# Key-tile order for the transposed image: packed reads for k and v, raster order restored in q's copy

## The chip, the cores and the metric

The kernel runs on one core of one Trainium2 chip. The metric is the device time of one execution in microseconds. A core has a matrix engine (TensorE, PE in the profile, with its weight loads listed as PEld), a vector engine (VectorE, DVE), an activation engine (ScalarE, ACT), a general engine (GpSimd, POOL) and SyncE (SP), which issues DMAs. Each engine works through its own queue in order; semaphores join them. A matmul takes a stationary operand, loaded into the array by its own instruction (LDWEIGHTS), and a moving operand that streams through; the result goes to PSUM[...].

## The reference

Eight images of 32 x 32 tokens with 384 channels go through two layers. Only the first layer is touched by the change; cut to what matters:

```python
# layer 0: group norm, then attention with 6 heads of 64 channels over all 1024 tokens of an image
qkv = gn(x).reshape(b, 1024, 384) @ qkv_w + qkv_b            # q, k, v per head
attn = (q * 64 ** -0.5) @ k.T                                # 1024 x 1024 per head
attn[h, w, h2, w2] += (q[h, w] . Rh[h, h2]) + (q[h, w] . Rw[w, w2])   # relative positions
x = x + (softmax(attn) @ v) @ proj_w + proj_b
# layer 1: x = x + causal attention(layer_norm(x)), then x = x + ffn(layer_norm(x))
```

The FFN quantises in groups along the batch, and only images 0 to 4 are in a group: images 5, 6 and 7 take no FFN. In softmax attention the order of the keys does not matter, as long as k, v and the position terms use the same one. The order of the queries shows in the output, and the position terms of layer 0 are made from q in raster order.

## The kernel before

**Stages.** Images are worked one after the other in `ORDER` = 5, 0, 1, 2, 3, 4, 6, 7. For each: group norm of the transposed image `gnT` (channels on partitions, 1024 tokens along the free side; `load_T`, `group_norm_T`), `layer0` (q, k, v, position tables), `attend0_fast` (scores, exponentials, values), the projection, then `attention1` and, for images 0 to 4, `ffn`. The time of a group norm of the next image, and of its first two thirds of q, falls into the layers of the current one: `ffn` calls `project_qk` for the image that follows, so that images 1, 2, 3, 4 and 6 find the results of q for the first two head pairs in PSUM. A tile framework puts buffers and semaphores in; the order on each engine is the order in the code, bent by `issue_after`, `behind_of` and `in_turn` (which chains matmuls).

**Keys in key tiles.** A tile of 128 keys is not 128 neighbours in raster order. Tokens are grouped in 256s, and tile (g, n) holds the tokens g * 256 + 2 * i + n, i from 0 to 127: the even or the odd columns of eight rows. This fits the position terms: `unit` and `r` (L913 to L916) add both terms of a tile with one matmul per head.

**q.** `queries_keys(m)` (L716 to L732), for m = 0 to 2, copies two halves of 512 tokens from PSUM to `q`, with scale and bias: half 0 on ACT (L732), half 1 on DVE (L730); in the first image both are on ACT. `tables` (L738) multiplies q with the relative positions (L746), in raster order. `spread` and `place` (L760, L786) bring the tables by DMA and by two DVE subtractions (L794) to the rows `r`; of the DMAs of L800 half are issued by SP, half by POOL.

**k and v.** They are made by 15 products each instead of 18 (`ProductSet`, L612): each product multiplies a sum of image parts with a sum of weight parts (`xf`, `wf`), 128 channels by 512 tokens, and adds into one of six PSUM banks A to F. Some of the partial states are copied by ACT to SBUF pages `u` (L643, L647), four are combined there (L663), and when a bank is full, `final` adds or subtracts the kept part and writes the result: `put_keys` (L822 to L825) for k, `put_values` (L827 to L829) for v, both on DVE. For k the weights are stationary and 512 tokens stream. For v the roles are turned, since v is wanted with keys on partitions: the image tile is stationary and the weights `wf` stream, four tiles of 128 keys per product (`tiles=by_keys`, L633 to L636). In the profile the matmuls of both carry L578 and the names f_pr_A to f_pr_F; those of v have `wf` first. Layer 1 makes its q and v by the same products (f_pr_1q, f_pr_1v), with tiles of 128 neighbouring tokens.

As the image lies in raster order, key tiles are gathered with a step of two tokens where v reads it:

```python
def by_keys(x):
    keys = x.rearrange("p (g i n) -> p g n i", g=2, n=2)
    return [keys[:, j // 2, j % 2] for j in range(4)]
```

and `put_keys` sorts k into key tiles when it writes, so that the scores (L909) read packed tiles of k. Its innermost step goes over n, 128 elements of 4 bytes apart.

**The first image.** POOL makes the sums of layer 1's weights (`layer1_forms`, L197 to L219) in two parts. The second is issued after the last DMA of `place` that POOL issues for head pair 0 (L991 to L993). After v's products a small activation (L865) reads one of the pages and opens the exponentials (L918 to L920); the scores take PSUM banks as `put_values` gives them free.

Of the kernel before, what the change touches and what calls it, by code (L numbers as in the profile page):

```python
# [19 lines left out]
P = 128  # L20
B, H, W, C = 8, 32, 32, 384
T = H * W
NJ = T // P
NC = C // P
# [67 lines left out]
def conv_attn_hybrid(  # L92
# [19 lines left out]
    nc = tc.nc  # L112
# [21 lines left out]
    wqkv_sb = wf.rearrange("p r s o -> p (r s o)")[:, : NC * 3 * C].rearrange("p (k o) -> p k o", k=NC)  # L134
# [286 lines left out]
    def stages(pools):  # L421
# [151 lines left out]
        def behind_of(ins):  # L573
            return contextlib.nullcontext() if ins is None else tc.issue_after(ins)
# [111 lines left out]
        def project_qk(b, xT, m, w):  # L686

            made = [pools.o_tile(f"qk_{b}_{m}_{half}") for half in range(2)]
            for half in range(2):
                for i in range(NC):  # L690
                    (in_turn if pools.fast else nc.tensor.matmul)(
                        made[half], w[:, i, ts(m, P)], xT[:, i, ts(half, 512)], start=(i == 0), stop=(i == NC - 1)
                    )
            return made

        def layer0(b, xT):


            q, k = (pools.image(f"{n}_{b}") for n in ("q", "k"))
# [16 lines left out]
            def queries_keys(m):  # L716
                p = m % NPAIR
                bias = bqk[:, m : m + 1]
                made = ahead.pop((b, m)) if (b, m) in ahead else project_qk(b, xT, m, plain[0])
                for half, ps in enumerate(made):  # L720
                    t = ts(half, 512)
                    if m < NPAIR:
                        dst = q[:, p, t]
                    else:
                        dst = k[:, p, t].rearrange("d (g n i) -> d g i n", n=2, i=P)
                        ps = ps.rearrange("d (g i n) -> d g i n", n=2, i=P)
                    scale = qscale if m < NPAIR else 1.0
                    if half and not (pools.fast and b == ORDER[0]):
                        with behind_of(last_ended[0] if pools.fast else None):
                            last_ended[0] = nc.vector.tensor_scalar(dst, ps, scale, bias, ALU.mult, ALU.add).ins  # L730
                    else:
                        nc.scalar.activation(dst, ps, AF.Identity, bias=bias, scale=scale)  # L732
# [76 lines left out]

            v = pools.flat(f"v0_{b}")[:, : NJ * C].rearrange("p (j c) -> p j c", j=NJ)  # L810

            keys = xT.rearrange("p k (g i n) -> p k g n i", n=2, i=P)

            def values(j):
                ps = pools.o_tile(f"v0_{b}_{j}")[:, :C]
                for i in range(NC):
                    nc.tensor.matmul(
                        ps, keys[:, i, j // 2, j % 2], wqkv_sb[:, i, 2 * C :], start=(i == 0), stop=(i == NC - 1)
                    )
                (nc.vector.tensor_copy if j % 2 else nc.scalar.copy)(v[:, j, :], ps)  # L820

            def put_keys(ps, kept, p, half, op):  # L822
                dst = k[:, p, ts(half, 512)].rearrange("d (g n i) -> d g i n", n=2, i=P)
                ps, kept = (t.rearrange("d (g i n) -> d g i n", n=2, i=P) for t in (ps, kept))
                return nc.vector.tensor_tensor(dst, ps, kept, op).ins  # L825

            def put_values(ps, kept, p, half, op):  # L827
                ps, kept = (t.rearrange("t (j c) -> t j c", j=4) for t in (ps, kept))
# [2 lines left out]
            near = []  # L831

            def by_keys(x):
                keys = x.rearrange("p (g i n) -> p g n i", g=2, n=2)
                return [keys[:, j // 2, j % 2] for j in range(4)]

            def products():

                forms = xf.pop(b)
                of_k = ProductSet(f"{b}_1", forms, wf[:, :, 0, :], bias=True)  # L840
                of_v = ProductSet(f"{b}_2", forms, wf[:, :, 1, :], tiles=by_keys)
                parts = unfinished.pop() if unfinished else (lambda *js: None)
                queries_keys(0)
                queries_keys(1)
                near.append(positions(0))
                parts(0, 1)
                queries_keys(2)
                parts(2, 3)
                near.append(positions(1))
                parts(4, 5)  # L850
                parts(6, 7)
                of_k.run(5, put_keys)
                last_tables = tables(NPAIR - 1)
                of_k.run(3)
                with behind_of(of_k.last_copy):
                    of_k.behind = round_off(0, *near[0])
                of_k.run(N_PROD - of_k.at)
                with behind_of(of_k.last_copy):
                    of_v.behind = round_off(1, *near[0])
                with behind_of(place(0, *near[0], (None, last_ended[0]), rounded=True)):  # L860
                    near.append(spread(NPAIR - 1, *last_tables))
                of_v.run(N_PROD, put_values)
                early = pools.small.tile([P, 1], F32, tag="early", name=f"early0_{b}")
                with behind_of(of_v.last_copy):
                    exp_loaded[0] = nc.scalar.activation(early, of_v.part["n5"][:, 0:1], AF.Exp, scale=0.0).ins  # L865

            if pools.fast:
                products()
            else:
                for m in range(2 * NPAIR):  # L870
                    queries_keys(m)
                    if 0 < m <= NPAIR:
                        near.append(positions(m - 1))
                    if m == NPAIR and unfinished:
                        unfinished.pop()(*range(NJ))
                for j in range(NJ):
                    values(j)
                place(0, *near[0])
# [567 lines left out]
        def run(pools):  # L1446
# [39 lines left out]
            if pools.fast:  # L1486
# [6 lines left out]
                with tc.issue_after(last_scaled[0]):  # L1493
                    next(join, None)
                    make_fold()
            for b in ORDER:
                xt, more = layer0(b, gn)

                def between():
# [85 lines left out]
```

## Time and profile before

| what | value |
|---|---|
| median of three runs | 2267.55 us (2267.29 to 2268.35) |
| the profiled execution's own time | 2271.02 us |
| its span | 2269.2 us |
| PE busy | 2257.0 us (99%) |
| PE weight loads busy | 1387.8 us (61%) |
| DVE busy | 1633.2 us (72%) |
| ACT busy | 1208.3 us (53%) |
| POOL busy | 527.2 us (23%) |
| granted TensorE clock | 0.999 of full |

Times in the profile are microseconds from the span's start, single instructions' means in nanoseconds. A line of the groups has the source line, engine and operation, out<-in by the program's names, the shapes and the count; then busy time and mean; then the engine's idle time just before them and what ended it. A line of the timeline has start, duration, engine, source line, operation, and in brackets the idle time before it and its releaser. An fp32 matmul stands in the records as two, each with its weight load, and the end of a matmul is modelled: the pace of a stream is read from starts.

### The profile page before, as it was taken

What the parts mean: (1) busy time and instruction counts of PE and PEld (TensorE: products, weight loads), DVE (VectorE), ACT (ScalarE), POOL (GpSimd) and SP (SyncE); (2) the same over time, 40 slices, a digit from 0 to 9 for tenths busy, and PEclk for the clock granted to TensorE, in tenths of its full rate; (3) what the DMA queues carried; (4) which work ended last, traced back from release to release, by engine and by line L of the source; (5) the groups of instructions that cost most, each with busy time, mean ns of one, the idle gap of its engine ahead of it and who ended that gap; (6) DMA issues with size and microseconds to landing.
All of it is one profiled execution on the core that took longest, in us unless ns stands there. A gap on an engine that the chain in (4) does not pass through costs nothing.

```text
span 2269.2 us, 30149 instructions
## 1 busy us (share of the span) xinstructions
PE 2257.0 (99%) x10597; PEld 1387.8 (61%) x10597; DVE 1633.2 (72%) x2746; ACT 1208.3 (53%) x2181; POOL 527.2 (23%) x696
## 2 busy tenths in 40 slices
PE   9999999999999999999999999999999999999998
PEld 4547554768645677547685475874477754755475
DVE  6898578875888548886468884588864788727882
ACT  4654266337664457654476543767444766317541
POOL 7512222230131401312102313013040131221310
PEclk9999999999999999999999999999999999999999
DMA  6530562140740205520308202074102372016200
GB/s 192 146 93 28 159 139 55 47 163 29 150 104 29 73 40 120 127 65 1 112 30 186 67 29 108 21 153 111 31 5 107 73 170 60 10 47 153 56 1 30
DMA packets 182048, 188.50 MB, mean 83 GB/s; under 512 B 138763, under 2 KB 151488, under 8 KB 179072
## 3 DMA queue, kind: packets, MB, share of 16 engines
q1 hardware_dynamic: 163680, 115.80, 20.9%
q0 software_dynamic: 17376, 69.30, 9.8%
q8 instruction: 87, 1.43, 0.3%
q10 hardware_dynamic: 832, 1.38, 0.2%
q14 instruction: 73, 0.60, 0.1%
HBM read 84.52 MB, written 51.56 MB: 60 GB/s over the span
## 4 chain that ended last, share of the span: by engine, by line
PE 99%; DVE 0%; DMA 0%; SPq 0%; issue 0%; ACT 0%
PE f_s L909 15%; PE f_av L935 15%; PE f_av L1218 8%; PE f_s L1204 8%; PE f_y L1412 7%; PE f_y L1362 7%; PE f_qk L578 6%; PE f_s L913 4%; PE f_pr_A L578 4%; PE f_pr_B L578 3%; PE f_pj L1026 3%; PE f_pj L524 3%; PE f_rel L578 2%; PE f_pr_1v_A L578 2%; PE f_pr_1q_A L578 2%; PE f_pr_1v_B L578 2%
## 5 line engine op out<-in xcount | busy, mean ns | idle before, releaser
L920 ACT ACTIVATE f_pr<-f_s 128x512 f32<-128x512 f32 x768 | 412.4, 595 | 40.8 <-PE f_s L913 36.3
L909 PE MATMUL f_s<-f_q,f_k 64*128 64x512 f32 x1536 | 400.6, 595 | 2.4 <-DVE f_v L829 2.4
L927 DVE TENSOR_TENSOR f_sum<-f_sum,f_pr 128x1024 f32<-128x1024 f32 x288 | 368.0, 1278 | 25.9
L935 PE MATMUL f_av<-f_pr,f_v 128*64 128x512 f32 x1536 | 340.2, 595 | 0.0
L913 PE MATMUL f_s<-f_r,unit 64*128 64x512 f32 x768 | 310.0, 792 | 0.0
L935 PEld LDWEIGHTS f_av<-f_pr,f_v 128*64 128x64 f32 x1536 | 106.0, 137 | 218.3 <-issue 191.9
L909 PEld LDWEIGHTS f_s<-f_q,f_k 64*128 64x128 f32 x1536 | 148.0, 186 | 127.0 <-issue 66.5
L1204 PE MATMUL f_s<-f_q,f_lnT 128*128 128x512 f32 (+3 forms) x576 | 198.3, 488 | 0.0
L1218 PE MATMUL f_av<-f_v,f_pr 128*128 128x385 f32 (+1 forms) x576 | 195.4, 486 | 0.0
L800 POOL DMA_DIRECT2D f_r<-f_far x192 | 102.2, 535 | 389.9 <-DVE f_far L794 175.7
L1218 PEld LDWEIGHTS f_av<-f_v,f_pr 128*128 128x128 f32 x576 | 108.1, 190 | 77.0 <-issue 11.5
L1213 ACT ACTIVATE f_pr<-f_s 128x512 f32<-128x512 f32 (+3 forms) x96 | 47.0, 491 | 203.1 <-DVE f_s L1209 160.2
L1204 PEld LDWEIGHTS f_s<-f_q,f_lnT 128*128 128x128 f32 x576 | 100.7, 190 | 70.0 <-issue 46.9
L1373 DVE TENSOR_REDUCE am<-f_h 128x1 f32<-128x1024 f32 (+2 forms) x80 | 71.6, 946 | 95.6 <-ACT f_h L1366 95.6
L1366 ACT ACTIVATE f_h<-f_y,biases 128x256 f32<-128x256 f32 x240 | 100.8, 471 | 66.8 <-PE f_y L1362 66.8
L913 PEld LDWEIGHTS f_s<-f_r,unit 64*128 64x128 f32 x768 | 76.3, 187 | 88.7 <-issue 88.5
L578 PE MATMUL f_qk<-f_gnT,wq_sb 128*128 128x512 f32 x288 | 127.9, 595 | 0.0
L1412 PE MATMUL f_y<-f_w2a,f_hilo 128*128 128x384 f32 x640 | 127.2, 341 | 0.0
L1007 ACT COPY f_oT<-f_av 128x512 f32<-128x512 f32 x40 | 23.5, 587 | 190.4 <-PE f_av L935 190.4
L1412 PEld LDWEIGHTS f_y<-f_w2a,f_hilo 128*128 128x128 f32 x640 | 112.5, 188 | 3.8 <-issue 1.4
L925 DVE TENSOR_TENSOR f_sum<-f_pr,f_pr 128x1024 f32<-128x1024 f32 x48 | 62.2, 1295 | 71.8 <-ACT f_pr L920 71.8
L1316 POOL PARTITION_ALL_REDUCE qa<-qg x10 | 3.7, 367 | 459.1 <-DVE qg L1314 459.1
(286 smaller groups left out, 4189.2 us busy)
## 6 DMA issues: line engine op xcount, KB each, us to landing
f_far<-f_far SPq DMA_DIRECT2D x48, 512.0 KB, 4.6
f_r<-f_far SPq DMA_DIRECT2D x192, 128.0 KB, 3.0
f_r<-f_far POOLq DMA_DIRECT2D x192, 128.0 KB, 4.5
f_far<-f_far SPq DMA_DIRECT2D x192, 64.0 KB, 4.7
f_x<-in_x SPq DMA_DIRECT2D x32, 384.0 KB, 4.7
f_gnT<-in_xT SPq DMA_DIRECT2D x21, 512.0 KB, 4.8
f_w1a<-w1s POOLq DMA_DIRECT2D x5, 1536.0 KB, 6.6
f_w2a<-w2s POOLq DMA_DIRECT2D x5, 1536.0 KB, 8.2
```

The lines of the kernel that those rows point to most:

```text
L578: last_product[0] = nc.tensor.matmul(*args, **kw).ins
L800: put = (nc.gpsimd if i else nc.sync).dma_start(out=r(part, p).bitcast(F32).rearrange("(m i) t -> i m t", i=4)[2 * i + d], in_=pages[i][ts ...
L909: nc.tensor.matmul(sc[par], k[rows[par], p, ts(c, P)], q[rows[par], p, ts(half, 512)], start=True, stop=False)
L913: last_matmul[0] = nc.tensor.matmul(sc[par], unit[rows[par], c // 2 % 2].rearrange("i h w -> i (h w)"), r(2 * (c // 4) + c % 2, p)[rows[pa ...
L920: last_exp[0] = nc.scalar.activation(pr[:, ts(par, 512)], sc[par], AF.Exp).ins
L927: adds.append(nc.vector.tensor_tensor(total, total, pr, ALU.add).ins)
L935: last_matmul[0] = nc.tensor.matmul(av[ts(par, HD), :], v[:, c, ts(2 * p + par, HD)], pr[:, ts(par, 512)], start=(c == 0), stop=(c == NJ - 1),
L1204: last_score[0] = nc.tensor.matmul(sc[:, lo:], xT[:, c // 4, k, ts(c % 4, P)], q[:, half, k, lo:], start=(k == 0), stop=(k == NC - 1),).ins
L1218: made = nc.tensor.matmul(av, prs[c][:, ts(j - c, P)], what(c), start=(c == 0), stop=(c == j)).ins
L1362: nc.tensor.matmul(ps, w1k[i // 2][:, ts(m, P)], xs[i % 2][:, half, i // 2, :], start=(i == 0), stop=(i == 2 * NC - 1))
L1366: nc.scalar.activation(pairs[i][:, m, :, :], ps[:, ts(i % 2, 256)].rearrange("p (j q) -> p j q", j=2), AF.Identity, bias=b1_sb[:, m : m + 1],)
L1412: nc.tensor.matmul(ps[:, :C], h, w, start=(i == 0), stop=(i == len(products) - 1))
```

## The change

The array `xT` that the host gives is laid out in key-tile order: within each group of 256 tokens first the 128 even ones, then the 128 odd ones. Everything that reads it follows: group norm is indifferent to the order, the sums of image parts are made as before. `by_keys` and `values` take 128 neighbours; `put_keys` writes where it reads. q comes out of PSUM in key-tile order, and `queries_keys` puts it back into raster order as it copies: it reads PSUM packed and writes with a step of two tokens. Line numbers behind the edits move up by five.

```diff
 # queries_keys
                     if m < NPAIR:
-                        dst = q[:, p, t]
+                        dst = q[:, p, t].rearrange("d (g i n) -> d g n i", n=2, i=P)
+                        ps = ps.rearrange("d (g n i) -> d g n i", n=2, i=P)
                     else:
-                        dst = k[:, p, t].rearrange("d (g n i) -> d g i n", n=2, i=P)
-                        ps = ps.rearrange("d (g i n) -> d g i n", n=2, i=P)
+                        dst = k[:, p, t]
 # values
-            keys = xT.rearrange("p k (g i n) -> p k g n i", n=2, i=P)
-                        ps, keys[:, i, j // 2, j % 2], wqkv_sb[:, i, 2 * C :], start=(i == 0), stop=(i == NC - 1)
+                        ps, xT[:, i, ts(j, P)], wqkv_sb[:, i, 2 * C :], start=(i == 0), stop=(i == NC - 1)
 # put_keys
-                dst = k[:, p, ts(half, 512)].rearrange("d (g n i) -> d g i n", n=2, i=P)
-                ps, kept = (t.rearrange("d (g i n) -> d g i n", n=2, i=P) for t in (ps, kept))
-                return nc.vector.tensor_tensor(dst, ps, kept, op).ins
+                return nc.vector.tensor_tensor(k[:, p, ts(half, 512)], ps, kept, op).ins
 # by_keys
-                keys = x.rearrange("p (g i n) -> p g n i", g=2, n=2)
-                return [keys[:, j // 2, j % 2] for j in range(4)]
+                return [x[:, ts(j, P)] for j in range(4)]
 # given
-        "xT": np.asarray(x).reshape(B, T, C).transpose(0, 2, 1),
+        "xT": np.asarray(x).reshape(B, T // (2 * P), P, 2, C).transpose(0, 4, 1, 3, 2).reshape(B, C, T),
```

The keys' branch of `queries_keys` and `values` belong to a second path of the kernel, which runs if sums overflow, and not in the profiled execution.

## The prediction

> **What bounds the kernel.** I read the page first, then the groups by shape, the instruction timeline of single stages, and the chain.
>
> ```profile
> span 2269.2 us, 30149 instructions
> ...
> PE 2257.0 (99%) x10597; PEld 1387.8 (61%) x10597; DVE 1633.2 (72%) x2746; ACT 1208.3 (53%) x2181; POOL 527.2 (23%) x696
> ...
> PE 99%; DVE 0%; DMA 0%; SPq 0%; issue 0%; ACT 0%
> ```
>
> TensorE is busy 99% of the span and carries 99% of the chain. An edit counts if it changes the pace of TensorE's stream or one of the few waits in it. TensorE runs for itself in one edited place: the v products (`of_v`, bank names f_pr, weights operand wf moving, image tile stationary). The groups by shape set them beside the v products of layer 1 (f_pr_1v), which load packed tiles:
>
> ```profile
> L578 PEld LDWEIGHTS f_pr_1v_A<-w1f,f_xf 128*128 128x128 f32 x320 | 44.6, 192 | 5.1 <-issue 3.6 <-ACT f_u_1v L643 0.2
> L578 PEld LDWEIGHTS f_pr_A<-wf,f_xf 128*128 128x128 f32 x320 | 41.5, 196 | 3.8 <-issue 3.5 <-POOL w1f L197 0.2
> ...
> L578 PE MATMUL f_pr_1v_A<-w1f,f_xf 128*128 128x128 f32 x320 | 48.7, 275 | 0.0
> L578 PE MATMUL f_pr_A<-wf,f_xf 128*128 128x128 f32 x320 | 44.3, 281 | 0.0
> ```
>
> Same shape, same type, both operands 128 columns; the strided load takes 4 ns more and its matmul 6 ns more. Durations overlap, so the price is in the starts, which the timeline has (start, duration, count):
>
> ```profile
> 735.13 0.61 PE L578 MATMUL f_pr_1v_B<-w1f,f_xf 128*128 128x128 f32 x4
> ...
> 738.26 0.60 PE L578 MATMUL f_pr_1q_A<-f_xf,w1f 128*128 128x256 f32 x2
> ...
> 604.64 1.10 PE L578 MATMUL f_pr_E<-wf,f_gnT 128*128 128x128 f32 x8
> ...
> 608.41 0.87 PE L578 MATMUL f_pr_A<-wf,f_gnT 128*128 128x128 f32 x6
> ```
>
> Packed: seven products of 4 records lie between 735.13 and 738.26, so 3.13 us / 28 = 111.8 ns a record. Strided: four products of 8 records in 3.77 us, 117.8 ns. Each matmul appears as two records.
>
> The other place is a wait in image 5, the first processed, where TensorE stands for 2.43 us. The timeline of DVE, POOL, ACT and PE:
>
> ```profile
> 52.55 1.10 DVE L825 TENSOR_TENSOR f_k<-f_pr_A,f_u 128x512 f32<-128x512 f32 x1
> 53.47 3.22 DVE L794 TENSOR_TENSOR f_far<-f_far 64x1024 fp32r<-64x1024 f32 x2
> 56.99 3.68 POOL L800 DMA_DIRECT2D f_r<-f_far  x7 [1.13 <-DVE f_far L794]
> 60.69 1.42 POOL L197 TENSOR_TENSOR w1f<-f_raw 128x128 f32<-128x128 f32 x2
> 63.51 6.18 DVE L663 TENSOR_TENSOR f_u<-f_u 128x512 f32<-128x512 f32 x1 [0.74 <-ACT f_u L643]
> 68.69 1.31 POOL L197 TENSOR_TENSOR w1f<-w1f,f_raw 128x128 f32<-128x128 f32 x2
> 69.72 0.20 ACT L865 ACTIVATE early<-f_u 128x1 f32<-128x1 f32 x1 [4.94 <-DVE f_u L663]
> 70.47 0.69 PE L909 MATMUL f_s<-f_q,f_k 64*128 64x512 f32 x1 [2.43 <-DVE f_v L829]
> ```
>
> The last partial-sum subtraction (L663), 0.69 us elsewhere, lasts 6.18 and ends as POOL's run of weight forms ends, at 69.7-70.0. Behind it wait the small activation that opens the exponentials, and the put_values that free score banks.
>
> **What the Trainium skill says.** "SBUF — State Buffer", Door 1: SBUF lines are 16 bytes, and two hits per line give full rate. On that, fp32 at stride two should cost nothing; the trace differs for weight loads (117.8 against 111.8 ns), and the measurement decides. A stride of 512 bytes meets each line once: put_keys (L825) shows it. Same page, Who interferes with whom: a DVE instruction with two SBUF inputs and a GpSimd instruction reading SBUF exclude each other for whole instructions; L663's 6.18 us agrees in kind. "TensorE: Matmul & The Clock Gate", LDWEIGHTS: time goes with columns, 128/1.2 = 107 ns; 111.8 is near it, so the load sets the pace here.
>
> **The change part by part.**
>
> Stationary tiles of v packed: 15 products x 4 tiles x 2 records = 120 records an image, 960 in all, at 117.8 - 111.8 = 6.0 ns: 0.72 us an image, 5.8 us. Bounds: nothing, if the 6 ns is not the stride; 5.8 if it is. I take 5.8, since layer 1's products differ in no other operand shape. The seven later images carry 7 x 0.72 = 5.0; the first hides its 0.72 in the wait above if that stays. `values` (L814) is not run on this path.
>
> put_keys packed: 48 instructions, 6 an image. Groups:
>
> ```profile
> L825 DVE TENSOR_TENSOR f_k<-f_pr_A,f_u 128x512 f32<-128x512 f32 x8 | 8.9, 1113 | 0.0
> L829 DVE TENSOR_TENSOR f_v<-f_pr_A,f_u 128x512 f32<-128x512 f32 x8 | 5.4, 680 | 0.0
> ```
>
> L829 does the same sum with packed runs. About 0.4 us each leaves 48 x 0.4 = 19 us of DVE's 1633, of which the path sees nothing in images 2 to 8: TensorE keeps its 0.94 us product pitch there, and the f_pr_F load, which follows the first put_keys, has its own pitch (0.86 us) as cover. In the first image three of them stand in a row before L794. Their starts are 0.92 apart (50.72, 51.63, 52.55, 53.47), those of L829 0.61 (69.72, 70.33, 70.93): 3 x 0.31 = 0.93 us. The L663 before them stays where it is, tied to POOL until 50.14. L794, then the eight POOL DMA issues of L800 (order 55.25 to 60.67), then POOL's forms all move 0.93 earlier; the forms end 0.93 earlier, and so does L663, if it is again held to their end. SP's own issues of L800 hang on ACT and stay; POOL's eight rows land earlier by 0.93, while TensorE needs them 0.72 earlier, so cover grows.
>
> q copies scattered at stride two: 27 on ACT (L732, 687 ns) and 21 on DVE (L730, 750 ns). No row shows an 8-byte write stride. Lower end 0 more, upper end put_keys' 0.4 us at 512 bytes; below zero is excluded, packed being the best case. I take 0. Cover: in image 5 the q of pair 2 is ready at 34.16 and read at 39.76; in the five images made during the FFN two ACT copies (from 563.51) stand in the GELU stream, whose last low part ends at 568.23 and is read at 18/24 of 568.46 to 572.65, 571.6: over 3 us. At 0.4 x 2 it holds.
>
> Moves: on each engine the instructions keep their order; the DMA of the image keeps its shape, as the permutation is in the given array. Twelve matmuls gain a wait on TensorE's own counter, for matmuls at least 13 instructions back, finished by then: nothing. k is read as before, packed tiles.
>
> Sum for the first image: -0.93. Sum: -5.04 - 0.93 = -6.0 us on the profiled 2271.0 us (span 2269.2 and 1.8 around it). The median, 2267.55, is 3.5 below that execution; the difference carries over: **2261.6 us**.
>
> **Rivals and chances.**
>
> Forecast (0.42): packed pace, L663 still held to the forms' end. 2261.6, its own range 2260.9 to 2262.3.
>
> Released lock (0.30): POOL and DVE alternate, as at 40.56, 44.42 and 46.90, where L663 took only 0.92, 0.72 and 1.01. Scores start 8.93 us before the first av (611.40 to 620.33 in a later image); here 64.8 to 77.29 is 12.5, so 3.56 returns, plus the first image's 0.72: -5.04 - 4.28 = -9.3, 2258.2. For: only this L663 of 64 starved. Against: the new order is nearly the old one.
>
> Earlier collision (0.14): the L663 before (60.69) moves to about 60.2 by the faster products (11 x 0.048), the forms to 59.76; it is then the one held, to 69.07. Behind it queue two put_values, the last L663 and the opening activation: 69.1 + 0.7 + 0.65 + 0.6 + 0.7 = 71.8 against 69.72, +2.05. Total -3.0: 2264.6. For: it now arrives inside the forms. Against: it would arrive near their start, where DVE got in.
>
> No packing gain (0.09): the 6 ns belongs to something else (four tiles in a 512-wide bank against two in 256). Against: six 128-wide matmuls of L1204 on packed tiles last 0.83 us together (784.78), so (0.83 - 0.275) / 5 = 111 ns. Then -0.9 to -4.3 from the first image: about 2265.5.
>
> Slower (0.05): scattered q copies so slow that GELU is late in five images. With 3 us of cover and two ACT copies each, it begins at 1.5 us more per copy; it eats the 6 us from 2.1 more; at 3.0 more it costs 5 x (6.0 - 3.0) = 15, net +9: 2276.6. Nothing in the page shows more than 0.43.
>
> From these: 0.2% is 4.5 us, about what a measurement can tell from no change. Faster: forecast (nearly all) and released lock, 0.70; within: the collision and no packing, 0.25; slower 0.05. The range leaves out the slower case, most of no packing, and a little below: 2257.5 to 2265.
>
> **What would show it.** Right: LDWEIGHTS f_pr<-wf at 192 ns, MATMUL at 275, eight records in 0.89 us instead of 0.94; L825's successor about 690; L730 and L732 as before; POOL's forms from about 59.8. Wrong: 196 and 281 unchanged; q copies over 1.5 us longer; a DVE wait of TensorE outside the first image.

## The result and the profile after

The changed kernel takes 2261.99 us (median of 11 runs, 2261.66 to 2263.43) against 2267.57 us of the kernel before on the same chip (11 runs, 2267.22 to 2268.71): a ratio of 0.9976, 95% interval 0.9968 to 0.9984. That is 5.58 us less. 2261.6 us had been forecast, so the number was met; the reason for it was only partly the one given.

The head of the page of the changed kernel, and the shares of its chain:

```profile
span 2260.7 us, 30149 instructions
...
PE 2251.2 (100%) x10597; PEld 1380.3 (61%) x10597; DVE 1613.0 (71%) x2746; ACT 1208.5 (53%) x2181; POOL 526.9 (23%) x696
...
PE 99%; DMA 0%; DVE 0%; SPq 0%; issue 0%
```

TensorE lost 5.8 us of busy time (2257.0 before; in a second pair of profiles, described below, 2256.2 and 2251.2, 5.0 us), VectorE 20 us (1633.2 before; in the second pair 1633.9 and 1620.8, 13 us). TensorE carries the chain alone as before, so only the first of these can be seen in the time.

The groups by shape of the changed kernel, the v products and one of put_keys:

```profile
L578 PE MATMUL f_pr_A<-wf,f_xf 128*128 128x128 f32 x320 | 42.7, 276 | 0.0
L578 PEld LDWEIGHTS f_pr_A<-wf,f_xf 128*128 128x128 f32 x320 | 39.5, 192 | 3.9 <-issue 3.6 <-POOL w1f L197 0.2
...
L821 DVE TENSOR_TENSOR f_k<-f_pr_D,f_u 128x512 f32<-128x512 f32 x8 | 5.5, 692 | 0.7
```

The load takes 192 ns (196 before) and the matmul 276 (281), as layer 1's packed products; put_keys takes 680 to 692 ns where it took 1.06 to 1.11 us. In the chain a v product of eight records lasts 0.89 us instead of 0.94.

The first image looks quite different. The timeline of VectorE, in the changed kernel, at the place where L663 lasted 6.18 us before:

```profile
63.50 0.93 DVE L663 TENSOR_TENSOR f_u<-f_u 128x512 f32<-128x512 f32 x1 [0.17 <-ACT f_u L643]
64.46 0.69 DVE L825 TENSOR_TENSOR f_v<-f_pr_C,f_u 128x512 f32<-128x512 f32 x1
```

and what POOL did meanwhile:

```profile
63.17 0.28 POOL L219 COPY w1f<-f_raw 128x128 f32<-128x128 f32 x1
63.43 1.30 POOL L197 TENSOR_TENSOR w1f<-f_raw 128x128 f32<-128x128 f32 x2
```

L663 waits 0.2 us, the pair of POOL's sums pays for it (1.30 us instead of 0.86), and TensorE's wait for f_v, 2.4 us in the first profile of before, is gone. The two profiled spans therefore differ by 8.5 us (2269.2 and 2260.7), 3 us more than the medians do. That was the first thing to explain.

### The profile page after: what moved, and what is told of

It reads as the page before. It is cut to its first block, busy times and chain, and to the rows that moved or that the text cites. A ratio compares the mean times of both kernels' runs of the same rounds, so it can differ in the third digit from the quotient of the medians.

```text
span 2260.7 us, 30149 instructions
## 1 busy us (share of the span) xinstructions
PE 2251.2 (100%) x10597; PEld 1380.3 (61%) x10597; DVE 1613.0 (71%) x2746; ACT 1208.5 (53%) x2181; POOL 526.9 (23%) x696
## 4 chain that ended last, share of the span: by engine, by line
PE 99%; DMA 0%; DVE 0%; SPq 0%; issue 0%
PE f_s L904 15%; PE f_av L930 15%; PE f_av L1213 8%; PE f_s L1199 8%; PE f_y L1407 7%; PE f_y L1357 7%; PE f_qk L578 6%; PE f_s L908 4%; PE f_pr_A L578 4%; PE f_pr_B L578 3%; PE f_pj L1021 3%; PE f_pj L524 3%; PE f_rel L578 2%; PE f_pr_1v_A L578 2%; PE f_pr_1q_A L578 2%; PE f_pr_1v_B L578 2%
```

## The experiments

**The parts, one at a time.** Three kernels take one edit each from the change, applied to the kernel before; a fourth keeps the code of before and makes the collision of the last L663 and POOL's second run of forms impossible.

```diff
 # e1_v_packed: by_keys
-                keys = x.rearrange("p (g i n) -> p g n i", g=2, n=2)
-                return [keys[:, j // 2, j % 2] for j in range(4)]
+                return [x[:, ts(j, P)] for j in range(4)]
 # e2_k_packed: put_keys
-                dst = k[:, p, ts(half, 512)].rearrange("d (g i n) -> d g i n", n=2, i=P)
-                ps, kept = (t.rearrange("d (g i n) -> d g i n", n=2, i=P) for t in (ps, kept))
-                return nc.vector.tensor_tensor(dst, ps, kept, op).ins
+                return nc.vector.tensor_tensor(k[:, p, ts(half, 512)], ps, kept, op).ins
 # e3_q_step2: queries_keys
-                        dst = q[:, p, t]
+                        dst = q[:, p, t].rearrange("d (g i n) -> d g n i", n=2, i=P)
+                        ps = ps.rearrange("d (g n i) -> d g n i", n=2, i=P)
 # e4_forms_gated: attend0_fast (the lines that pass `early` on and make the tile `gate` are left out)
                     with tc.issue_after(last_row[0]):
+                        gated = nc.gpsimd.tensor_copy(gate, exp_loaded_to[0]).ins
+                    with tc.issue_after(gated):
                         layer1_forms(pools, raw1[0], 1)
```

> The kernel before with one part of the change alone: the stationary tiles of the v products are packed 128-token blocks of the raster image. Keys of v then come in another order than those of k, so what is computed is another attention; the work is the same. Packing theory (the 6.0 ns of a record are the stride): loads at 192 ns, eight records in 0.89 us, seven to eight images of 0.72 us, so 5.0 to 5.8 us less: 2261.8 to 2262.6. First-image theory (what the change gains is the held subtraction L663, freed by earlier POOL work): packed tiles alone bring at most the first image's 0.7 us: 2266.8 to 2267.6.

> The kernel before with put_keys alone writing packed (k then lies in raster order while v keeps key-tile order, so another attention is computed, with the same work). Packing theory: VectorE loses 19 us of busy time, put_keys takes about 690 ns, and the time moves by at most the first image's 0.93 us: 2266.6 to 2267.6. First-image theory: it carries the gain, by the earlier POOL work: 3 to 5.6 us less, 2262 to 2264.6.

> The kernel before with the copies of q alone written at a step of two elements, from packed reads of PSUM (queries then come in an order of their own within every 256; the work is the same). If they are hidden: ScalarE's copies go from 687 to about 719 ns, VectorE's stay at 750, and the time stays within 0.5 us of the kernel before, 2267.1 to 2268.1. If they stand on the path in the five images made during the feed-forward part: two copies each, 5 x 2 x 0.03 = 0.3 us more; a larger loss, 1 us and up, would mean that the change hides a loss in its -5.6.

> The kernel before with POOL's second run of weight forms begun by a copy of one element of the opening activation's output, so that it starts only after the last L663 of the first image, and can't hold it. If the 6.18 us of L663 in the profiled execution stand in the timed runs too, 3 to 3.6 us come back: 2264 to 2264.6. If they were a matter of that one execution (its time, 2271.0, is 3.5 us over the median), the timed runs have nothing to give: 2267.1 to 2268.1, and L663 takes 0.7 us in the profile with the exponentials starting about 3.5 us earlier than in the profiled execution of before.

| kernel | median, us (range, runs) | ratio to before, 95% interval |
|---|---|---|
| before, same chip | 2267.51 (2267.06 to 2272.66, 57) | |
| e1, v packed | 2267.47 (2265.43 to 2268.93, 21) | 0.9995 (0.9988 to 1.0002) |
| e2, k packed | 2269.71 (2267.03 to 2270.43, 13) | 1.0001 (0.9993 to 1.0009) |
| e3, q scattered | 2267.44 (2266.96 to 2272.24, 13) | 1.0002 (0.9993 to 1.0010) |
| e4, forms gated | 2268.56 (2267.26 to 2274.38, 21) | 1.0008 (1.0002 to 1.0015) |

The ratio is not the quotient of the two medians; where the runs of a kernel fall into two groups, as those of e2 do, the two differ (1.0010 by the medians). By the medians, no part alone makes the kernel faster.

For e1 this contradicts the packing theory in the time and confirms it in the profile. Its chain:

```profile
52.59 0.89 PE f_pr_C L578 x8
...
62.46 0.60 ACT f_u L643
63.05 0.02 issue
63.08 6.32 DVE f_u L663
```

The products run at the packed pace, and then L663 is held for 6.3 us. POOL's timeline beside it, in e1:

```profile
62.96 0.45 POOL L197 TENSOR_TENSOR w1f<-w1f,f_raw 128x128 f32<-128x128 f32 x1
...
63.85 0.86 POOL L197 TENSOR_TENSOR w1f<-f_raw 128x128 f32<-128x128 f32 x2
...
68.39 1.31 POOL L197 TENSOR_TENSOR w1f<-w1f,f_raw 128x128 f32<-128x128 f32 x2
```

The pair at 63.85 keeps its 0.86 us, so it let nobody in; the last pair, 1.31 instead of 0.86, shows L663 coming through. All 21 runs of e1 lie above 2265.4 us, so none looks free of the hold. What the hold costs e1, and what its packing earns, the next experiment measures.

e2 shows the same hold, 4.89 us, at a time of 2270.0; three of its 13 runs stand at 2267.0 to 2267.3 and look free of it. Its VectorE does lose 15 us of work (1618.7 us), with no gain; its median lies above both of its forecasts. e3 is hidden, as reckoned.

In e4 L663 takes 0.69 us and the exponentials start early, and still half of its runs stand at 2267.3 to 2268.1, about the median of before: the median run of before has no hold to lose, it seems. Ten of e4's 21 runs stand at 2270 to 2274 and lift its median above both forecasts; which wait that is no profile shows. Its own profile shows the lock the other way round, POOL held by VectorE's sums of exponentials: pairs of forms that take 0.86 us elsewhere last

```profile
70.17 2.84 POOL L197 TENSOR_TENSOR w1f<-w1f,f_raw 128x128 f32<-128x128 f32 x2
72.97 2.83 POOL L197 TENSOR_TENSOR f_wsum<-f_raw 128x128 f32<-128x128 f32 x2
```

**Packing without the collision.** To see what packing is worth by itself, POOL's second run of weight forms is moved far away from the v products, behind the last multiplication of oT in the first image.

```diff
-                    with tc.issue_after(last_row[0]):
-                        layer1_forms(pools, raw1[0], 1)
+                    pass
 ...
-                        nc.gpsimd.tensor_tensor(oT[:, p0, t0], oT[:, p0, t0], rb, ALU.mult)
+                        multiplied = nc.gpsimd.tensor_tensor(oT[:, p0, t0], oT[:, p0, t0], rb, ALU.mult).ins
+                        if b == ORDER[0] and (p, half) == (NPAIR - 1, 0):
+                            with tc.issue_after(multiplied):
+                                layer1_forms(pools, raw1[0], 1)
```

e4b is the kernel before with it, e12 is e1 with it, e5b the changed kernel with it. e11 also moves the first run there, from the k products.

> The kernel before with packed stationary tiles of v, as in e1 (keys of v in another order than those of k), and POOL's second run of weight forms moved from the start of the first image's scores to behind the last oT multiplication of that image, so that no L663 of the first image's v products can be held by it. If e1's gain of 5.0 us on seven images was eaten by the held L663 of the first (6.31 us in its profile), the whole packing gain of 5.0 to 5.8 us now shows: 2261.8 to 2262.6. If packing is worth nothing in the time, 2267 to 2268, as e1.

> The kernel before with the same move of POOL's second run of weight forms, and nothing else. If most timed runs of the kernel before do not have the held L663 and a few do (7 of 57 stood at 2272), the median stays at 2267.2 to 2267.8 and the runs at 2272 are gone. If they all have it, 3 to 3.6 us come back: 2264 to 2264.6. If the runs at 2272 have another cause, they stay.

> The changed kernel with the same move of POOL's second run of weight forms. If its timed runs are already free of the held L663: 2261.5 to 2262.5, as the changed kernel. If some of its gain is still locked: 3 us less.

> The changed kernel with both runs of layer 1's weight forms on POOL moved behind the last oT multiplication of the first image (19 us of work from about 150, needed from 180.7), so that the k products' L663 meet none either. In the profile of the changed kernel four L663 of the k products last 0.69 to 0.91 us beside POOL, and none stands on the path; so 2261.5 to 2262.5, as the changed kernel; if they delay something, up to 0.7 us less; if POOL is then late for layer 1, more than 2262.5.

| kernel | median, us (range, runs) | ratio to before, 95% interval |
|---|---|---|
| before, same chip | 2267.36 (2266.94 to 2269.00, 45) | |
| e4b, before, forms late | 2268.67 (2268.22 to 2271.14, 13) | 1.0006 (0.9997 to 1.0014) |
| e12, v packed, forms late | 2263.24 (2262.70 to 2265.53, 17) | 0.9982 (0.9974 to 0.9989) |
| e5b, after, forms late | 2263.33 (2262.46 to 2265.18, 21) | 0.9982 (0.9976 to 0.9989) |
| e11, after, both late | 2277.93 (2276.82 to 2279.87, 5) | 1.0046 (1.0033 to 1.0060) |

Between e4b and e12 only the step of the stationary tiles differs, and both are free of the hold: 5.43 us, where 960 x 6.0 ns = 5.8 had been reckoned. Between e12 and e5b lie put_keys and the copies of q: 0.1 us, nothing. So all of the change's direct gain is the packed load of v.

e1's hold can now be priced: its first put_values of the second image starts at 299.69, that of e12 at 294.48, 5.2 us later. Some 1.5 us of this are the clock and not the wait. (The granted clock is the share of full speed at which TensorE was clocked.) In e1's profile it is 0.50 from 70 to 73 us, directly behind TensorE's wait, and the first matmul there lasts 1.22 us:

```profile
70.17 1.22 PE L908 MATMUL f_s<-f_q,f_k 64*128 64x512 f32 x1 [2.62 <-DVE f_v L829]
```

In the first profile of before the clock stays at 1.00 behind a wait of 2.43 us, and the same matmul lasts 0.69 us. Some 2.9 us of work at half clock, 70.17 to about 73.1, cost half of that, 1.5 us; the 3.7 us that remain are close to the 3.6 us which the hold turns out to cost before (below). That e1 ends at the median of before is therefore a coincidence of sizes: hold and clock together take what packing earns. Its four fastest runs, 2265.4 to 2266.4 us, would fit a hold without the loss of clock; they have no profile. Why the clock fell behind one wait and not behind the other, no run shows.

Moving the forms has a price of its own: e4b and e5b both lie 1.3 us above the kernel that they came from, and e12 and e5b miss their forecasts by 0.6 and 0.8 us for it. About 0.9 us of it lies behind the last instruction of the computing engines: from there to the end of the span it is 6.7 us in the repeated profiles of before and after (below), 7.6 us in e4b and e5b. The reason is open. In the comparison of e4b with e12 (7.7 us) it drops out. Whether the runs of before at 2272 go away with the forms moved, e4b could not show, since the 45 runs of before beside it have none above 2269.0. No version beats the changed kernel. e11 is 16 us slower than it, and in its profile not because POOL was late for layer 1. The waits of its TensorE begin with

```profile
PE f_den L964 <- DVE few L941: 13.0, 1, 13.0
```

and its VectorE timeline has the cause, a first sum of exponentials, a kind that takes 1.3 us in the mean of the changed kernel:

```profile
151.76 6.97 DVE L920 TENSOR_TENSOR f_sum<-f_pr,f_pr 128x1024 f32<-128x1024 f32 x1 [4.38 <-POOL w1f L197]
```

Both runs of POOL's forms stand in that stretch (to 166.8), and now the last sums of the image, with TensorE directly behind them, are what is held. Behind the wait the granted clock is low as well, 0.50 from 165 to 175 us and 0.70 in the 5 us after, while TensorE works again from 173.1. The hold is not a property of L663: here another sum of two SBUF operands on VectorE meets it.

**Again, and two sizes.** The last four: both kernels unchanged, to see whether the hold belongs to a kernel or to an execution; a step of four tokens for v's tiles; a wide step for q's copies.

```diff
 # e13_v_step4_late: by_keys of e5b
-                return [x[:, ts(j, P)] for j in range(4)]
+                keys = x.rearrange("p (i n) -> p n i", n=4)
+                return [keys[:, j] for j in range(4)]
 # e8_q_step128: queries_keys of after
-                        dst = q[:, p, t].rearrange("d (g i n) -> d g n i", n=2, i=P)
-                        ps = ps.rearrange("d (g n i) -> d g n i", n=2, i=P)
+                        dst = q[:, p, t].rearrange("d (g n i) -> d g i n", n=2, i=P)
+                        ps = ps.rearrange("d (g i n) -> d g i n", n=2, i=P)
```

> The kernel before, unchanged, profiled again. If the held L663 of its first profile is a matter of the single execution, this profile has it or not: at a time of 2267.5 the last L663 of the first image's v products takes 0.7 to 1.0 us, at a time of 2271 and more about 5 to 6 us. If it is always there, it takes 6 us at a time of 2267.5 as well. The timed runs: 2267.2 to 2267.8 in the median, some at 2272.

> The changed kernel, unchanged, profiled and timed again. If its order keeps the last L663 out of the hold, all runs stand at 2261.6 to 2263.5 and the profile shows 0.9 us; if the hold is only rarer, some runs stand 3.5 to 5 us higher, at 2265 to 2267.

> The changed kernel with POOL's second run of weight forms late, as in e5b, and with stationary tiles of v that take every fourth token of a 512-wide form (step of 16 bytes; keys of v then come in another order than those of k, the work is the same). If the price of a record grows with the step (each 16 bytes hold one element instead of two), a record costs clearly more than 117.8 ns: at twice the loss, 123.8 ns, the time is 960 x 12 = 11.5 us over e5b, about 2274.8. If a step costs 6 ns whatever its size, 117.8 ns and about 2268.7, as e4b. If step 4 is free and the 6 ns had another cause, 2263.3.

> The changed kernel with the copies of q written at a step of 128 elements (512 bytes, put_keys' old pattern) instead of two, from packed reads of PSUM (queries then come in an order of their own; the work is the same). By put_keys, VectorE's copies take about 0.4 us more, 1.15 us; ScalarE's anything from 719 ns to 1.1 us. If the feed-forward part covers two ScalarE copies an image, as reckoned (3 us), the time stays at 2261.5 to 2262.8; if they stand on the path, 5 x 2 x 0.4 = 4 us more, about 2266.

| kernel | median, us (range, runs) | ratio to before, 95% interval |
|---|---|---|
| before, same chip | 2267.43 (2267.16 to 2273.71, 26) | |
| e9, before again | 2267.53 (2267.03 to 2272.22, 13) | 1.0000 (0.9992 to 1.0009) |
| e10, after again | 2262.02 (2261.68 to 2262.26, 10) | 0.9975 (0.9966 to 0.9985) |
| e13, step four, forms late | 2378.62 (2378.47 to 2378.94, 5) | 1.0490 (1.0476 to 1.0505) |
| e8, q at 512 bytes | 2262.01 (2261.45 to 2262.72, 9) | 0.9976 (0.9966 to 0.9986) |

The second profile of before, at 2267.41 us, has no hold. VectorE's timeline:

```profile
63.38 0.90 DVE L663 TENSOR_TENSOR f_u<-f_u 128x512 f32<-128x512 f32 x1 [0.63 <-ACT f_u L643]
```

So the same instructions in the same order hold L663 in one execution and not in another, and the 2271.02 us of the first profile contain about 3.6 us that this execution, which stands at the median, does not have: the first put_values of the second image starts at 298.88 there and at 295.19 here. Between the repeated profiles, free of it on both sides, the gain grows evenly. Starts of the first put_values of an image (VectorE, from the PSUM tile of bank D):

| image | 1st | 2nd | 3rd | 4th | 5th | 6th | 7th | 8th | span |
|---|---|---|---|---|---|---|---|---|---|
| before again | 58.53 | 295.19 | 601.66 | 908.13 | 1214.57 | 1520.77 | 1827.23 | 2063.82 | 2265.7 |
| after again | 58.33 | 294.34 | 600.11 | 905.90 | 1211.66 | 1517.21 | 1822.93 | 2058.82 | 2260.3 |
| difference | 0.20 | 0.85 | 1.55 | 2.23 | 2.91 | 3.56 | 4.30 | 5.00 | 5.4 |

The difference grows by 0.65 to 0.74 us from each image to the next, the first image among them. The absolute starts scatter more (58.93 and 58.33 in the two profiles of after), so it is the steps that count.

e13 is the largest effect of the study: 115.3 us more than e5b. Its groups:

```profile
L578 PE MATMUL f_pr_A<-wf,f_xf 128*128 128x128 f32 x320 | 80.2, 394 | 0.0
L578 PEld LDWEIGHTS f_pr_A<-wf,f_xf 128*128 128x128 f32 x320 | 79.0, 328 | 2.9 <-issue 1.9
```

and a product in its chain:

```profile
54.20 1.87 PE f_pr_C L578 x8
```

1.87 us / 8 = 233 ns a record, against 117.8 at step two and 111.8 packed. 960 x (233 - 112) = 116 us, the whole difference. Only the step of the stationary operand differs from e5b, so here the load sets the pace of the stream. The prediction had put that forward from an estimate, 107 ns for a load of 128 columns. All three expectations were wrong, and the one that was nearest, a price that grows with the step, was ten times too small. "SBUF — State Buffer" of the Trainium skill (Door 1: The DMA port swizzle) has SBUF in lines of 16 bytes which want two hits each for full bandwidth. At step four there is one hit per line and the pace is twice as slow: that agrees in kind. At step two there are two, and the stream still loses 5%: there the measurement decides.

In e8 the copies of q are 0.4 us longer on both engines; ScalarE's, at 1.17 us, take a little more than the 1.1 us allowed for:

```profile
L732 ACT ACTIVATE f_q<-f_qk,biases 128x512 f32<-128x512 f32 x27 | 31.7, 1174 | 50.5 <-PE f_qk L578 50.5
L730 DVE TENSOR_SCALAR f_q<-f_qk,biases 128x512 f32<-128x512 f32 x21 | 22.8, 1127 | 21.0 <-PE f_qk L578 20.9
```

and the time is that of the changed kernel to 0.01 us: the cover that the prediction reckoned with holds for 0.45 us a copy. From 1.5 us on it was to be gone; that was not tried.

**When L663 gets in.** The eight profiles in which the forms keep their place and their start give the moment at which L663 asked, measured from the start of the pair of sums that follows the copy of L219 on POOL:

| profile | asked, us from that pair | L663 lasted, us |
|---|---|---|
| e1 | -0.77 | 6.31 |
| before, first profile | -0.64 | 6.18 |
| e3 | -0.35 | 0.91 |
| before again | -0.33 | 0.90 |
| after again | +0.06 | 0.95 |
| after, first profile | +0.07 | 0.93 |
| e8 | +0.08 | 0.91 |
| e2 | +0.64 | 4.89 |

It got in when it asked within about 0.35 us before that pair and 0.1 after it; earlier or later it stood until the last pair. Before lies at the edge, at -0.64 in one execution and -0.33 in another; packed v alone makes L663 earlier and packed k alone makes POOL earlier, each pushing it out of the gap on its side; together they leave it inside. That accounts for e1, e2 and the changed kernel. It would also account for the single runs of before around 2272 (9 of the 152 in these tables and the first comparison are above 2271) and for none above 2264 among the 30 of after, after again and e8. The nine lie at least 4.5 us above the median, more than the 3.6 us of the hold. But seven of them have a granted clock of 0.998, where the other runs of before have 0.999 or 1.000 as far as it is on record: a hold with a loss of clock as in e1, 3.6 + 1.5 us, would fit. None of this is shown, since those runs have no profile, and e4 has such times, most of them at 0.998 too, with no L663 to hold. Why the gap lies where it does is open: the add of e11 asked while POOL was in the copy of L215, as the L663 of before again did, and was held.

## Why the prediction came out right

**Packed stationary tiles: right.** 960 records at 6.0 ns, 5.8 us; 5.43 measured between e4b and e12, 5.4 to 5.6 between before and after. The load at 192 ns, the matmul at 276 (275 was said) and the 0.89 us product came out. "No packing gain" is excluded by e12.

**The first image: wrong.** The step that failed is "the difference carries over", from the profiled 2271.0 us to the median. It took the 6.18 us L663 for a part of every run. In the repeated profile of before, which stands at the median, there is no hold; the 3.5 us by which the profiled execution stood above the median were the hold itself, and the profile's own numbers said so (its time was 3.5 us over the median, and 3.56 us was the price worked out for the release). Two errors then nearly cancelled, so that the number came out by luck: -0.93 us was counted for POOL's forms, which do begin 0.83 us earlier (59.51 against 60.34 in the repeated profiles) but are worth nothing where nothing waits for them, and the first image's 0.72 us of packing was left out as hidden, where it counts like every other. Right would have been 8 x 0.72 = 5.76 and 2261.8; 2261.99 was measured.

**The cases.** Against the first profile of before, "Released lock" came true (8.64 us less between the two profiled executions, 9.3 said). Against the median the number of the likeliest case was met, with its mechanism, L663 still held, absent. "Earlier collision" did not occur in after: the L663 before the last lasts 1.12 us and gets in. But its point, that faster products move a subtraction into the forms, is what costs e1 its gain; it was applied to the wrong L663.

**put_keys: right that it is hidden**, 680 to 692 ns and 13 to 20 us less on VectorE for 0.1 us. It was not free of effect, though: without it POOL's forms come 0.8 us later relative to the last L663 (-0.77 against +0.07), and e1 shows what the packed v is then worth. The parts do not add: by the medians 0.0 for v, +2.2 for k (its ratio's interval still holds 1) and -0.1 for q, and -5.6 together.

**q copies: the size was off, the verdict right.** VectorE's stay at 750 ns. ScalarE's went from 687 to 719 ns at a step of 8 bytes, where 0 more had been taken, and it is hidden, e3 and e8 both show. **Waits of TensorE on its own counter:** put at nothing; the 5.4 to 5.6 us of the whole change against 5.43 of packing leave no visible room for them.

## What to carry to other kernels

A profile is one execution: where its time lies well above the median of the runs, look for the stall that makes the difference before carrying it into a sum. An edit that shifts two engines against each other can create or remove a collision worth as much as its gain, so its parts should be tried with the collision taken out. Strided stationary operands deserve a look: two fp32 apart cost 5% of a load-bound stream, four apart doubled it.

## What the runs showed that was not expected

- A weight load of 128 x 128 fp32 at a step of 16 bytes paces its records at 233 ns instead of 111.8.
- Behind a wait of TensorE of 2.62 us the granted clock was 0.50 for about 3 us (e1); behind one of 2.43 us it stayed at 1.00 (before, first profile). The wait then costs more than itself.
- A VectorE sum of two SBUF operands can be held through a run of some fifteen back-to-back GpSimd instructions (6.31 us in e1, 6.97 in e11), not for one; "SBUF — State Buffer", Who interferes with whom, describes the exclusion for the length of one instruction. In another execution of before L663 asked a third of a microsecond later and waited 0.2 us.
- It works both ways: in e4 GpSimd's pairs lasted 2.84 us instead of 0.86 beside VectorE's sums.
- Writes at a step of 512 bytes cost ScalarE 1170 ns against 687 packed, VectorE 1119 against 750; at 8 bytes 719 and 750.
